# A gather that waits for the scores of an earlier tile: sparse graph attention on Trainium2

## The chip, the cores and the metric

The kernel runs on one core of a Trainium2 chip. It uses all five engines of that core: PE (matmul), DVE (vector), ACT (scalar), POOL (general purpose, and the issuer of every indirect DMA here) and SP (the issuer of the plain DMAs). The metric is the device time of one execution in microseconds (us), taken as the median of the runs. Times inside an execution are from one profiled execution and count from its first instruction.

## The reference

Four graph-attention layers follow each other, each as `x = x + layer(relu(layernorm(x)), adj)`. `x` is (8, 2048, 64): batch of 8, 2048 nodes, 64 channels. `adj` is 2048 x 2048 and sparse; its first rows are the densest. The change is in the third layer, which has four heads and then a second attention over the heads' output:

```python
def _gat_layer(h, mask, b):
    scores = jnp.einsum('...nd,...md->...nm', h, h)
    scores = jnp.where(mask, scores, NEG)
    attn = jax.nn.softmax(scores, axis=-1)
    return jnp.einsum('...nm,...md->...nd', attn, h) + b

mask = graph + jnp.eye(N, dtype=graph.dtype) > 0
h = jnp.einsum('bnc,hdc->bhnd', x, Wh)                 # 4 heads
out_h = _gat_layer(h, mask[None, None], bh[None, :, None, :])
z = leaky_relu(concat of the heads, 0.2)
h2 = jnp.einsum('bnk,dk->bnd', z, Wo)
out2 = _gat_layer(h2, mask[None], bo)                  # one head over h2
out = layernorm(leaky_relu(out2, 0.2)) * gamma + beta
```

Layer 1 (counted from 0) and layer 3 are additive attentions, layer 0 is a dot-product attention.

## The kernel before, in words

The kernel never forms a 2048 x 2048 score matrix. A first stage turns `adj` into lists of edges. The nodes are cut into 16 tiles of 128. A tile's edges are held in **slots** of 128 edges each: `ROWS[i]` slots in which partition p holds a neighbour of the tile's own node p, and then `PACKED[i]` slots into which the edges that are left over are packed, with a selection matrix that says which node each belongs to. One slot costs one **gather**: an indirect DMA that POOL issues (L256, in `gather`), which fetches 128 rows of 512 floats (8 batches x 64) from a table in HBM into one place of a ring of `RING = 26` places in SBUF. A tile has 3 to 16 slots, and all 16 tiles together have 76.

The stage of the change is called **the heads**: the first attention of layer 2. Its tiles are worked through in `ORDER2 = [8, 9, 12, 10, 13, 11, 3, 7, 5, 6, 2, 4, 0, 14, 1, 15]`. I write T13.0 for slot 0 of tile 13. `pipeline` runs five functions per tile, staggered by one tile each:

- `take2` issues the gathers of a tile (POOL), the load of its own rows (`rows<-table`, SP, L265), the load of its queries for four heads (`q<-qtab`, SP, L808, 1040 KB; the first two tiles have it in SBUF already), and the first loads of queries per packed edge (`qe<-qtab,qidx`, an indirect DMA of POOL, L797, 1040 KB; four buffers).
- `first2` calls `score` twice, once for the `ROWS` slots and once for the packed ones. For each slot ACT copies the gathered row to PSUM (L820), DVE multiplies it with the query (L822, 128x2048) and reduces the product (L826), a small DVE operation subtracts the self score (L827), and ACT takes the exponential (L828). A packed slot needs its `qe` load; the next `qe` load is issued when a packed slot's L827 is done.
- `second2` sums the weights by node (PE, L438), and for each half of the heads (k = 0, 1) POOL multiplies each gathered row with its weights (`wh`, L839; L855 adds two of them in some tiles; three buffers), and PE accumulates the result (`y`, L857), starting from the tile's own rows (L848). ACT divides (L869). After this the tile's ring places are free.
- `third2` and `fourth2` transpose, project and write the rows for the next attention (PE L898, L902, L914, L920; ACT L900, L481, L917, L922; DVE L482).

What stands in which order on each engine is decided by a list scheduler when the program is built: it estimates times for the operations and their dependencies, and emits one fixed sequence for each engine. On the chip each engine then runs its sequence in that order; an instruction whose semaphore isn't there yet holds all that stand behind it on that engine. So a new dependency changes not only when an instruction may start but also where it stands, and the places of others with it. A gather that needs a ring place waits for the operations that read the place's last content.

`gather` has an argument `behind`: an instruction that the **first** gather of the tile (slot 0) has to wait for. The two additive layers use it already, with the tile `SPREAD[k]` (2 or 3) ahead. The heads pass nothing.

Of the kernel before, what the change touches and what calls it, by code (L numbers as in the profile page):

```python
# [13 lines left out]
OP = mybir.AluOpType  # L14
AX = mybir.AxisListType
# [54 lines left out]
def edge_stack(ctx: ExitStack, tc: tile.TileContext, x_in, adj, w1, w1t, a1, wh, wht, bh, wo, bo,  # L70
# [9 lines left out]
    nc = tc.nc  # L80
# [127 lines left out]
    def heads(t, n=B):  # L208
        return t.rearrange("p (b d) -> p b d", b=n)
# [7 lines left out]
    order = list(MAKING)  # L217
# [13 lines left out]
    kept = {}  # L231
# [12 lines left out]
    def row(i, t):  # L244
        return ring[:, (held[i] + t) % RING, :F]

    taken = {}

    def gather(k, i, st, behind=None):

        n = SLOTS[i]
        assert sum(SLOTS[j] for j in held) + n <= RING
        held[i], front[0] = front[0], (front[0] + n) % RING
        cols = table[k].shape[1]
        for t in range(n):
            g = nc.gpsimd.indirect_dma_start(  # L256
                out=ring[:, (held[i] + t) % RING, :cols], out_offset=None, in_=table[k][:, :],
                in_offset=bass.IndirectOffsetOnAxis(ap=idx[:, OFF[i] + t:OFF[i] + t + 1], axis=0))
            if behind is not None and t == 0:
                tc.add_manual_dep(g.ins, behind.ins.name, mybir.DependencyInfo(  # L260
                    mybir.DependencyClass.Sync, mybir.DependencyReason.DATA), reason="gather")

    def load(st, name, src, bufs):
        st[name] = rows_pool[0].tile([P, F], F32, name=name, bufs=bufs)
        nc.sync.dma_start(out=st[name], in_=src)  # L265

    def rows_of(k, i):
        return table[k][i * P:(i + 1) * P, :F]
# [512 lines left out]
    with tc.tile_pool(name="l2", bufs=2) as l2p, \  # L781
# [10 lines left out]
        def fetch(upto):  # L792

            while len(sent) <= min(upto, len(stream) - 1):
                i, t = stream[len(sent)]
                q = sent[i, t] = l2p.tile([P, QW], F32, name="qe", bufs=QE)
                nc.gpsimd.indirect_dma_start(  # L797
                    out=q, out_offset=None, in_=qtab[:, :],
                    in_offset=bass.IndirectOffsetOnAxis(ap=qidx[:, POFF[i] + t:POFF[i] + t + 1], axis=0))

        def take2(i, st):
            gather(2, i, st)
            load(st, "rows", rows_of(2, i), 3)
            if i in order[:2]:
                st["q"] = kept[i]
            else:
                st["q"] = own_pool[0].tile([P, QW], F32, name="q")
                nc.sync.dma_start(out=st["q"], in_=qtab[i * P:(i + 1) * P, :])  # L808
            fetch(stream.index((i, 0)) + min(PACKED[i], QE) - 1)

        def score(i, st, lo, hi):

            K, n = ROWS[i], hi - lo
            w = l2p.tile([P, max(ROWS), B * H], F32, name="w2", bufs=5)[:, :n]
            st.setdefault("w", []).append(w)
            s = ps_s.tile([P, F], F32, name="s2")[:, :n * B * H].rearrange("p (t c) -> p t c", c=B * H)
            for t in range(lo, hi):
                q = st["q"] if t < K else sent[i, t - K]
                g = ps_g.tile([P, F], F32, name="g2")
                nc.scalar.copy(g, row(i, t))  # L820
                pr = l2p.tile([P, B * H, D], F32, name="prod2")
                nc.vector.tensor_tensor(  # L822
                    pr.rearrange("p (b h) d -> p b h d", h=H),
                    q[:, :B * H * D].rearrange("p (b h d) -> p b h d", h=H, d=D),
                    heads(g)[:, :, None, :].to_broadcast([P, B, H, D]), op=OP.mult)
                nc.vector.tensor_reduce(s[:, t - lo, :], pr, AX.X, OP.add)  # L826
                nc.vector.tensor_tensor(s[:, t - lo, :], s[:, t - lo, :], q[:, B * H * D:], op=OP.subtract)  # L827
                nc.scalar.activation(w[:, t - lo], s[:, t - lo], AF.Exp, bias=mbb[:, OFF[i] + t:OFF[i] + t + 1])  # L828
                if t >= K:
                    fetch(stream.index((i, t - K)) + QE)  # L830
# [41 lines left out]

        def first2(i, st):
            score(i, st, 0, ROWS[i])
            score(i, st, ROWS[i], SLOTS[i])

        def second2(i, st):
            d, p = by_query(i, st["w"], B * H)
            rec = st["rec"] = small.tile([P, B, H], F32, name="rec2")
            rf = rec.rearrange("p b h -> p (b h)")  # L880
            nc.vector.scalar_tensor_tensor(rf, p, 1.0, d, op0=OP.add, op1=OP.add)
            nc.vector.tensor_reduce(most2[:, i:i + 1], rf, AX.X, OP.max)
            nc.vector.reciprocal(rf, rf)
            for k in range(2):
                weights(i, st, k)
                divided(i, st, k)
            done(i, st)
# [42 lines left out]
    with tc.tile_pool(name="ps_q", bufs=3, space=bass.MemoryType.PSUM) as ps_q, \  # L930
# [88 lines left out]
        lo = small.tile([1, 1], F32, name="lo", bufs=1)  # L1019
# [514 lines left out]
```

## Time and profile before

| | |
|---|---|
| time, median of 3 runs | 1483.09 us |
| the three runs | 1474.09, 1483.09, 1483.28 us |
| the profiled execution | 1474.39 us, of which the span of its instructions is 1472.7 us |
| mean granted TensorE clock in it | 0.906 |
| busy in it | PE 1197.5 us, DVE 1153.7, POOL 1041.3, ACT 729.5 |
| gathers (L256), all layers | 380, mean 962 ns of POOL each |
| query loads per packed edge (L797) | 34, mean 963 ns of POOL each |
| `wh` products (L839) | 152, mean 1917 ns |
| score product and reduction (L822, L826) | 76 each, 2.28 us each |
| the heads, from the first gather to the last matmul | 529.9 to about 1053 us |

How to read it: POOL's 0.96 us for an indirect DMA is the time to issue it; the data land later, by semaphore. Busy time of PE is of pipelined matmuls, so a PE that is busy all the time needn't be at its peak. The window view gives for each stretch of time the busy time of each engine, the granted clock, the share of the 16 DMA engines that is busy, and what they move. The timeline gives single instructions in order, with the idle time before each and what ended it. The chain is the sequence of work that ended last, followed back from the end.

### The profile page before, as it was taken

The page shows a single profiled execution, that of the slowest core. Times are in us where ns is not written, and L with a number is a line of the kernel's source. Part 1 is how long each engine was busy: PE and PEld are TensorE (multiplying, and loading weights), DVE is VectorE, ACT ScalarE, POOL GpSimd, SP SyncE. Part 2 cuts the span into 40 slices and gives each one's busy share as a digit, 9 for nine tenths or more (in the row PEclk, how much of TensorE's full clock was granted, in tenths as well). Part 3 has the DMA queues.
Part 4 walks back from the last instruction along what each step waited for, and adds up shares of the span by engine and source line. Part 5 has one row for each costly group of instructions (what it writes and reads, how often), then busy time and mean ns, then how long its engine had stood idle before and what let it go on. Part 6 is the DMA issues. An engine that isn't in the chain of part 4 may idle for free.

```text
span 1472.7 us, 16011 instructions
## 1 busy us (share of the span) xinstructions
PE 1197.5 (81%) x4106; PEld 634.3 (43%) x4106; DVE 1153.7 (78%) x2267; ACT 729.5 (50%) x2467; POOL 1041.3 (71%) x851
## 2 busy tenths in 40 slices
PE   4757887957999852988999989988767798957997
PEld 1733444544554421444444434443333354555654
DVE  6978998735779896989888998951279999955765
ACT  5636677853445731666654654343524547741111
POOL 4646888857863558888787999987288689727640
PEclk9997999977999976999999999999868879957999
DMA  7767665537874578755455436200284453138861
GB/s 227 265 200 259 188 219 172 198 112 227 288 230 156 217 287 296 238 188 203 157 196 166 144 125 236 66 7 8 81 300 144 131 176 122 66 120 234 253 188 46
DMA packets 88621, 262.76 MB, mean 178 GB/s; under 512 B 14828, under 2 KB 16792, under 8 KB 80200
## 3 DMA queue, kind: packets, MB, share of 16 engines
q0 software_dynamic: 35680, 136.59, 29.6%
q1 hardware_dynamic: 52840, 125.06, 24.4%
q8 instruction: 35, 0.57, 0.2%
q14 instruction: 66, 0.54, 0.1%
HBM read 204.41 MB, written 57.18 MB: 178 GB/s over the span
## 4 chain that ended last, share of the span: by engine, by line
PE 29%; DVE 16%; POOL 7%; issue 6%; DMA 6%; ACT 5%; SPq 0%; DVEq 0%; POOLq 0%; ACTq 0%
PE y L857 9%; PE y L424 6%; DVE prod L822 4%; DVE s L826 3%; POOL g L256 3%; POOL wh L839 3%; PE y L848 2%; DMA g<-table,idx 2%; DMA rows<-table 2%; PE m L914 2%; PE m L902 2%; ACT yn L869 2%; DMA qe<-qtab,qidx 1%; PE q L606 1%; PE m L438 1%
## 5 line engine op out<-in xcount | busy, mean ns | idle before, releaser
L256 POOL DMA_INDIRECT g<-table,idx x380 | 365.4, 962 | 207.9 <-issue 80.3
L839 POOL TENSOR_TENSOR wh<-g,w 128x1024 f32<-128x1024 f32 x152 | 287.8, 1917 | 41.1 <-PE y L857 39.6
L424 PE MATMUL y<-wg,ident 128*128 128x512 f32 x336 | 192.5, 697 | 26.1 <-POOL wg L419 22.2
L826 DVE TENSOR_REDUCE s<-prod 128x32 f32<-128x2048 f32 x76 | 172.5, 2285 | 10.3 <-ACT w L828 10.1
L419 POOL TENSOR_TENSOR wg<-g,w 128x1024 f32<-128x1024 f32 (+1 forms) x86 | 146.6, 1719 | 31.7 <-ACT w L476 23.4
L857 PE MATMUL y<-wh,ident 128*128 128x512 f32 x272 | 133.9, 618 | 25.1 <-POOL wh L855 23.6
L424 PE MATMUL y<-wg,selt 128*128 128x512 f32 x272 | 141.0, 628 | 5.2 <-DVE wg L419 2.8
L857 PE MATMUL y<-wh,selt 128*128 128x512 f32 x272 | 128.4, 599 | 1.0 <-POOL wh L839 1.0
L869 ACT ACTIVATE yn<-y,rec 128x64 f32<-128x64 f32 x512 | 112.3, 370 | 23.6 <-DVE y L862 16.3
L424 PEld LDWEIGHTS y<-wg,ident 128*128 128x128 f32 x336 | 66.8, 217 | 97.5 <-issue 54.7
L419 DVE TENSOR_TENSOR wg<-g,w 128x1024 f32<-128x1024 f32 (+1 forms) x86 | 92.9, 1088 | 10.8 <-PE y L424 9.4
L438 PEld LDWEIGHTS m<-w,selt 128*128 128x128 f32 x408 | 63.6, 204 | 86.4 <-issue 23.7
L438 PE MATMUL m<-w,selt 128*128 128x8 f32 (+1 forms) x408 | 61.4, 255 | 47.3 <-ACT w L590 19.4
L822 DVE TENSOR_TENSOR prod<-q,g 128x2048 f32<-128x2048 f32 x42 | 95.6, 2276 | 3.0 <-ACT g L820 2.8
L468 PE MATMUL q<-rows,sel 128*128 128x512 f32 x136 | 80.9, 690 | 19.4 <-DVE prod L462 12.7
L822 DVE TENSOR_TENSOR prod<-qe,g 128x2048 f32<-128x2048 f32 x34 | 77.5, 2279 | 23.5 <-DMA qe<-qtab,qidx 16.8
L857 PEld LDWEIGHTS y<-wh,ident 128*128 128x128 f32 x272 | 52.1, 199 | 89.6 <-issue 57.7
L820 ACT COPY g<-g 128x512 f32<-128x512 f32 x76 | 47.6, 626 | 86.4 <-DVE prod L822 84.4
L424 PEld LDWEIGHTS y<-wg,selt 128*128 128x128 f32 x272 | 52.4, 205 | 60.1 <-issue 49.0
L902 PE MATMUL m<-att,whd 128*128 128x512 f32 x120 | 64.5, 619 | 15.0 <-ACT att L900 14.8
L857 PEld LDWEIGHTS y<-wh,selt 128*128 128x128 f32 x272 | 49.6, 190 | 60.8 <-issue 55.7
L482 DVE SCALAR_TENSOR_TENSOR zt<-m,bhc,att 128x512 f32<-128x512 f32 x60 | 44.4, 741 | 36.6 <-ACT att L481 36.6
(247 smaller groups left out, 2659.9 us busy)
## 6 DMA issues: line engine op xcount, KB each, us to landing
qtab<-q SPq DMA_DIRECT2D x16, 1040.0 KB, 4.8
a<-in_adj_dram SPq DMA_DIRECT2D x32, 512.0 KB, 5.0
q<-qtab SPq DMA_DIRECT2D x14, 1040.0 KB, 5.9
table<-xh SPq DMA_DIRECT2D x48, 256.0 KB, 3.7
rows<-table SPq DMA_DIRECT2D x48, 256.0 KB, 4.0
xs<-x SPq DMA_DIRECT2D x48, 256.0 KB, 2.5
x<-xs SPq DMA_DIRECT2D x48, 256.0 KB, 3.0
table<-xh SPq DMA_DIRECT2D x32, 260.0 KB, 2.4
```

The source lines that it names most:

```text
L256: g = nc.gpsimd.indirect_dma_start(out=ring[:, (held[i] + t) % RING, :cols], out_offset=None, in_=table[k][:, :], in_offset=bass.IndirectO ...
L419: eng.tensor_tensor(wg[:, :m].rearrange("p t (b d) -> p t b d", b=B), g[:, :, :F].rearrange("p t (b d) -> p t b d", b=B), w[:, t0:t0 + m, ...
L424: nc.tensor.matmul(y, lhs(i, t), wg[:, t - t0, :], start=(t == 0 and own is None), stop=(t == n - 1))
L438: nc.tensor.matmul(p[:, :cols], selt(i, t), packed[:, t, :], start=(t == 0), stop=(t == T - 1))
L468: nc.tensor.matmul(qe, sel(i, t - K), q, start=True, stop=True)
L820: nc.scalar.copy(g, row(i, t))
L822: nc.vector.tensor_tensor(pr.rearrange("p (b h) d -> p b h d", h=H), q[:, :B * H * D].rearrange("p (b h d) -> p b h d", h=H, d=D), heads(g ...
L826: nc.vector.tensor_reduce(s[:, t - lo, :], pr, AX.X, OP.add)
L839: nc.gpsimd.tensor_tensor(wg, heads(row(i, t))[:, :, None, :].to_broadcast([P, B, 2, D]), w[:, :, 2 * k:2 * k + 2, None].to_broadcast([P, ...
L857: nc.tensor.matmul(st["ys"][j], lhs(i, t), wg[:, 4 * j:4 * j + 4], start=first, stop=(t == n - 1))
L869: nc.scalar.activation(yn[:, b, h, :], st["ys"][j][:, b, h, :], AF.Copy, scale=st["rec"][:, 4 * j + b, 2 * k + h:2 * k + h + 1])
L902: nc.tensor.matmul(p, whd[j // 2], yt, start=True, stop=True)
```

## The change

In the heads, the first gather of a tile now waits for the scores of the tile that is four places ahead of it in `ORDER2`: for that tile's last reduction (L826) over its `ROWS` slots. Tiles 0 to 3 of the order wait for nothing more than before. The other gathers of a tile get no such wait. No operation is added or taken away, and no transfer changes its size.

```diff
         def take2(i, st):
-            gather(2, i, st)
+            n = order.index(i)
+            gather(2, i, st, taken[2, order[n - 4]] if n >= 4 else None)
             load(st, "rows", rows_of(2, i), 3)
...
-                nc.vector.tensor_reduce(s[:, t - lo, :], pr, AX.X, OP.add)
+                kept["s"] = nc.vector.tensor_reduce(s[:, t - lo, :], pr, AX.X, OP.add)
...
         def first2(i, st):
             score(i, st, 0, ROWS[i])
+            taken[2, i] = kept["s"]
             score(i, st, ROWS[i], SLOTS[i])
```

`gather` itself, unchanged, hangs the wait on slot 0 alone:

```python
            if behind is not None and t == 0:
                tc.add_manual_dep(g.ins, behind.ins.name, mybir.DependencyInfo(
                    mybir.DependencyClass.Sync, mybir.DependencyReason.DATA), reason="gather")
```

## The prediction

> **What bounds the kernel now.** The change touches one stage, so I looked for what holds that stage. First the window view, for the engines' load by stretch:
>
> ```profile
> core 0: us, PE busy (x) PEld busy (x) DVE busy (x) ACT busy (x) POOL busy (x), PEclk, DMA share, GB/s
> ...
> 558.00:571.00 13.00, 0.00 (x0) 0.00 (x0) 0.00 (x0) 0.00 (x0) 10.86 (x11) 0.50 0.94 345
> 571.00:600.00 29.00, 19.34 (x46) 8.86 (x46) 28.60 (x21) 10.91 (x38) 24.45 (x16) 0.82 0.66 233
> 600.00:625.00 25.00, 25.00 (x68) 10.77 (x68) 24.93 (x25) 15.41 (x57) 22.17 (x16) 1.00 0.74 255
> ```
>
> The reader is to see a hole: from 558 to 571 us PE, DVE and ACT do nothing at all; only POOL issues, and the DMA engines are 94% busy. After that PE and DVE are nearly full (600 to 900 us: PE 92 to 95%, DVE 88 to 94%, POOL 79 to 91%). The wait view of 500 to 620 us names the hole, and the chain of 556 to 592 us, in order of time, shows what it is made of:
>
> ```profile
> DVE prod L822 <- DMA qe<-qtab,qidx: 13.3, 1, 13.3
> ```
>
> ```profile
> 557.00 0.21 DVE s L827
> 557.21 0.29 issue
> 557.50 0.95 POOL g L256
> 558.45 0.30 issue
> 558.75 0.95 POOL g L256
> 559.70 0.30 issue
> 560.00 0.95 POOL g L256
> 560.95 0.30 issue
> 561.25 0.95 POOL g L256
> 562.21 0.30 issue
> 562.51 8.54 DMA qe<-qtab,qidx
> 571.05 0.02 issue
> 571.07 2.30 DVE prod L822
> ```
>
> POOL issues 26 gathers in a row (529.9 to 562.2 us, 1.25 us apart), until the ring's 26 places are used up, and only then the first `qe` load. DVE finished tile 8's three row slots at 557.2 and needs that load for slot T8.3. It lands 8.5 us after its issue began. Everything later in the heads hangs on this start.
>
> **What the change does to the order.** The orders of the two built programs show it on POOL: 22 gathers, then the four `qe` loads. T13.0, T11.0, T3.0 and T7.0 have left the opening run; T13.1, T13.2 and so on stay in it, since only slot 0 waits. T13.0 now stands between the second and third `wh` product of tile 8, T11.0 between T8.0 and T8.1 of its second half, T3.0 behind tile 8's last product, T7.0 before tile 12's third. Later slot 0s stand one to four places behind their sisters. DVE, ACT, PE and SP swap neighbours here and there, and in the next attention too. No work is added.
>
> **The opening.** Four gathers at 1.25 us are 5.0 us that the `qe` load gains on POOL: issue at 557.5 instead of 562.5. None of its semaphores holds it there: its youngest store to the query table was issued at 542.0, and it waits for a reduction ended at 541.9. What can take gain back is the landing. From 534 to 572 us the DMA engines are about full (0.82 to 1.02 in slices of 2 to 4 us), and SP issues a 1040 KB `q` load at 557.2, which the earlier `qe` load now has beside it from its first byte. The trace has no `qe` load at that instant; the five issued between 555 and 580 us landed in 6.2 to 11.1 us, median 9.8. So DVE resumes between 563.7 and 568.6, a gain of 7.4 to 2.5 us. I take the median of these neighbours: 557.5 + 9.8 = 567.3, a gain of **3.8 us**.
>
> The Trainium skill (DMA: Bandwidth & Descriptors, Anatomy of one DMA — SWDGE (gpsimd) path) fits an undisturbed load as 2.0 us plus bytes over 436 GB/s, an estimate of 4.4 us for these 1040 KB, where this trace shows 8.54; by it the gain would be 571.07 - 561.9, 9.1 us. The same page (Queues, rings and completion order) says that an engine takes turns between queues, packet by packet; that speaks against the full gain, as SP's load would get every other turn.
>
> **The gathers put back.** They cost 1.25 us of POOL each, in the middle of products. T13.0 stands ahead of the sum that PE's first product waits for: that sum ends 5.0 - 1.25 = 3.75 us earlier instead of 5.0 (575.15 now), which is what DVE gains anyway. T11.0: POOL's sum of T8.0 and T8.1 ends at 590.30, PE starts on it at 591.67, so 1.25 of 1.37 us slack are used. T8.3's product ends at 595.9, PE takes it at 597.4; still covered. T9.0's ends at 600.2 against 601.2 on PE, so up to 0.25 us late; the order lets POOL catch up one gather there (T6.0 stands later than before). T7.0 and T5.0 fall ahead of POOL's wait of 4.23 us for PE at 637.45. I take **0.3 us** for all of them; if POOL's cover were gone it would be 3 x 1.25 = 3.75 us, and below nothing isn't excluded by more than POOL's one spare gather, 1.25 us.
>
> **The waits added.** At a gather's new place, would POOL come before the reduction? By the timelines of before (reduction's end; POOL's arrival): T11.0 580.2; 583.0. T3.0 594.4; 595.9. T7.0 617.4; 619.9. T5.0 636.0; 633.6. T6.0 644.2; 645.6. T2.0 668.4; 669.6. T4.0 702.8; 700.1. So two waits, 2.4 and 2.7 us. Behind each stand gathers or `wh` products, and PE waits for these. But both fall where POOL sat idle for PE, 4.23 us at 637.45 and 4.89 us at 708.58, so they cost nothing; uncovered, 5.1 us. As DVE and POOL both move by about the same amount, the margins of 1.2 to 2.8 us should hold. From T0.0 on the pipeline's own waits come later than the new one.
>
> **The rest.** An earlier start passes through PE, full from 600 us on, to the end of the heads at 1053 us. PE's idle time between 571 and 1053 us is 37 us, and other places of `zt` (L482) on DVE may shift some of it. In the next attention DVE is 94 and 97% busy (1100 to 1200, 1200 to 1300 us), so another order there has 9 us of idle DVE time to gain or lose; SP's moved `q` load passes a `rows` load that isn't needed for some 40 us. I count all this as 0, within -3 to +3 us.
>
> **Sum:** -3.8 + 0.3 + 0 = **-3.5 us**. Against the profiled execution, 1474.39 - 3.5 = 1470.9 us. That execution agrees with the fastest of the three runs (1474.09); the other two are 9 us higher, at 1483.1 and 1483.3, without anything that the page could show of them. The predicted median carries the difference over: 1483.09 - 3.5 = **1479.6 us**.
>
> **Rivals.**
> 1. *The gain is swallowed.* POOL is 23.0 to 24.3 us busy of 25 from 825 to 975 us and has the same work as before, only moved; if the four gathers come back where POOL sets the pace, its end stays. For it: the high load there, and that POOL, with PE, ends the heads. Against: POOL idled 39.6 us waiting for `y` products between 565 and 1060 us, time that can hold 5. The same result if the `qe` load lands no earlier because DMA alone decides. 0 us: 1483.1.
> 2. *The load flies.* The `qe` load lands in 6.2 us, the shortest of its neighbours: -7.4 us, 1475.7. For it: four gathers, 1 MB, fewer in the rings ahead of it. Against: the `q` load beside it.
> 3. *Slower: POOL waits in front of products.* One mechanism, at T5.0 and T4.0 and at the margins under 1.5 us (T3.0, T6.0, T2.0): POOL, having lost its four opening gathers sooner than DVE regains its pace, reaches the gather before the reduction, and the products behind it come late to PE. Price: 2.4 + 2.7 us at the two, 3 x 1.25 us for gathers ahead of products, together 8.9, less the 3.8 of the opening: +5, 1488. It decides once PE has no stock of products left, that is, where POOL no longer waits for PE.
> 4. *It doesn't do what it says*, since other waits cover it: excluded at the opening by the built order; it is part of the first rival.
>
> **How the numbers follow.** Forecast 0.50, first rival 0.22, second 0.12, third 0.16. From the bounds, -7.4 on the faster group (1474.1) gives 1466.7, +5 on the slower group (1483.3) gives 1488.3; with the +-3 us of other orders I give 1466 to 1489. A measurement of this kernel can hardly tell less than 1% (14.8 us) from no change, and the runs themselves lie 9 us apart. Under -1% lies only the second rival in the faster group, and a little of the rest: 0.10. Over +1% lies none of the cases, only an accident of order larger than I can find: 0.08. Within: 0.82.
>
> **What would show it.** Right: 22 gathers ahead of the first `qe` load; DVE's wait for `qe` down from 13.3 to some 9.5 us; the last matmul of the heads 3 to 4 us earlier against the first gather; no wait of L256 for L826 above 3 us. Wrong: the wait for `qe` still 12 or more (DMA decides); POOL idle before L256 for L826 in several places and PE idle for `wh` grown by as much (third rival); heads equal and the difference in the next attention (orders).

## The result, and the profile after

The changed kernel is slower: 1491.1 us median (1479.25 to 1506.05) against 1479.21 us (1471.86 to 1491.39) for the kernel before, 20 runs each; the ratio is **1.0076, 95% interval 1.0050 to 1.0102**. It leaves out the longest run of the changed kernel (1506.05 us) as a slow one. The forecast was 3.5 us faster. The profiled execution of the changed kernel took 1499.93 us, its span 1498.2 us. That is near the upper end of its runs, and the profiled one of before (1474.39 us) is near the lower end: the two profiles differ by 25.5 us, twice what the medians do.

All lines from 803 on stand one to three lines lower in the changed kernel: the score product is L823, its reduction L827, the subtraction behind it L828, the `wh` product L840, `y` L858, and PE's L914 is L917.

The wait for the query load, in the wait view from 506 to 626 us (the heads start 5.8 us later in this execution, at 535.7 us, after stages whose order is the same in both kernels):

```profile
engine line waited for: us in total, times, longest us
...
DVE prod L823 <- DMA qe<-qtab,qidx: 8.8, 1, 8.8
```

The same instants on POOL, in its timeline:

```profile
start us, us, engine line op out<-in xcount [idle before <-releaser]
562.06 0.95 POOL L256 DMA_INDIRECT g<-table,idx  x1 [0.30 <-issue]
563.31 0.94 POOL L797 DMA_INDIRECT qe<-qtab,qidx  x1 [0.30 <-issue]
...
568.01 3.78 POOL L840 TENSOR_TENSOR wh<-g,w 128x1024 f32<-128x1024 f32 x2
```

The opening did what was forecast. The first `qe` load is issued 27.6 us after the first gather instead of 32.6, it lands 10.4 us later instead of 8.5, DVE's wait falls from 13.3 to 8.8 us, and the product of T8.3 starts 3.1 us earlier against the first gather. POOL's first product starts 5.0 us earlier, at 32.3 us instead of 37.3.

The windows that answer to those shown of before:

```profile
core 0: us, PE busy (x) PEld busy (x) DVE busy (x) ACT busy (x) POOL busy (x), PEclk, DMA share, GB/s
564.00:577.00 13.00, 0.00 (x0) 0.00 (x0) 3.77 (x5) 0.88 (x2) 11.89 (x9) 0.59 0.95 347
577.00:606.00 29.00, 23.39 (x52) 10.55 (x53) 28.13 (x26) 12.67 (x47) 23.62 (x18) 0.77 0.70 264
606.00:631.00 25.00, 24.02 (x63) 9.73 (x62) 24.56 (x21) 13.76 (x47) 19.16 (x13) 1.00 0.63 217
```

The second row holds the gain: PE does 52 matmul instructions in it where before did 46. The third row shows that it goes at once: PE does 63 instead of 68, and POOL is busy for 19.2 us instead of 22.2. POOL waits there. Its wait view over the whole heads, first of before (529.9 to 1060 us), then of the changed kernel (535.7 to 1072 us):

```profile
POOL wh L839 <- PE y L857: 39.6, 22, 4.9
```

```profile
POOL wh L840 <- PE y L858: 45.1, 23, 8.0
```

POOL does not wait for the scores that the change names: no gather of the heads has a wait for a reduction above 0.3 us. It waits longer for PE. Against the first gather, POOL's products stand 5.0 us earlier at tile 8, 0.5 us earlier at the end of tile 9, then 1.9 us later in the second half of tile 12, 4.1 us later in that of tile 11, 6.6 us later in that of tile 2, and so to the end. The stretch from the first gather of the heads to the first gather of the second attention is 535.7 us instead of 529.5. The second attention took 265.8 us instead of 260.8, the last layer 161.0 instead of 152.5.

### The profile page after: what moved, and what is told of

Same layout as the page of the kernel before. It is cut to its first block, busy times and chain, and to the rows that moved or that the text cites. A ratio compares the mean times of both kernels' runs of the same rounds, so it can differ in the third digit from the quotient of the medians.

```text
span 1498.2 us, 16006 instructions
## 1 busy us (share of the span) xinstructions
PE 1211.3 (81%) x4106; PEld 641.2 (43%) x4106; DVE 1149.7 (77%) x2267; ACT 728.9 (49%) x2467; POOL 1041.8 (70%) x851
## 5 line engine op out<-in xcount | busy, mean ns | idle before, releaser
L840 POOL TENSOR_TENSOR wh<-g,w 128x1024 f32<-128x1024 f32 x152 | 288.0, 1917 | 46.6 <-PE y L858 45.1
L424 PE MATMUL y<-wg,ident 128*128 128x512 f32 x336 | 190.4, 690 | 27.1 <-POOL wg L419 23.7
L827 DVE TENSOR_REDUCE s<-prod 128x32 f32<-128x2048 f32 x76 | 172.9, 2287 | 12.6 <-ACT w L829 12.4
L858 PE MATMUL y<-wh,ident 128*128 128x512 f32 x272 | 138.3, 636 | 19.2 <-POOL wh L856 17.8
L424 PE MATMUL y<-wg,selt 128*128 128x512 f32 x272 | 140.7, 627 | 5.1 <-DVE wg L419 4.3
L858 PE MATMUL y<-wh,selt 128*128 128x512 f32 x272 | 128.9, 600 | 0.0
L424 PEld LDWEIGHTS y<-wg,ident 128*128 128x128 f32 x336 | 66.7, 217 | 96.6 <-issue 54.7
L823 DVE TENSOR_TENSOR prod<-q,g 128x2048 f32<-128x2048 f32 x42 | 95.6, 2276 | 4.6 <-ACT g L821 4.4
L858 PEld LDWEIGHTS y<-wh,ident 128*128 128x128 f32 x272 | 53.3, 204 | 85.6 <-issue 58.1
L823 DVE TENSOR_TENSOR prod<-qe,g 128x2048 f32<-128x2048 f32 x34 | 77.4, 2277 | 15.2 <-DMA qe<-qtab,qidx 9.0
L424 PEld LDWEIGHTS y<-wg,selt 128*128 128x128 f32 x272 | 51.8, 203 | 58.8 <-issue 46.8
L858 PEld LDWEIGHTS y<-wh,selt 128*128 128x128 f32 x272 | 49.4, 190 | 61.9 <-issue 56.3
L482 DVE SCALAR_TENSOR_TENSOR zt<-m,bhc,att 128x512 f32<-128x512 f32 x60 | 44.4, 741 | 40.8 <-ACT att L481 40.7
```

What stands on the lines that cost most here:

```text
L424: nc.tensor.matmul(y, lhs(i, t), wg[:, t - t0, :], start=(t == 0 and own is None), stop=(t == n - 1))
L823: nc.vector.tensor_tensor(pr.rearrange("p (b h) d -> p b h d", h=H), q[:, :B * H * D].rearrange("p (b h d) -> p b h d", h=H, d=D), heads(g ...
L827: kept["s"] = nc.vector.tensor_reduce(s[:, t - lo, :], pr, AX.X, OP.add)
L840: nc.gpsimd.tensor_tensor(wg, heads(row(i, t))[:, :, None, :].to_broadcast([P, B, 2, D]), w[:, :, 2 * k:2 * k + 2, None].to_broadcast([P, ...
L858: nc.tensor.matmul(st["ys"][j], lhs(i, t), wg[:, 4 * j:4 * j + 4], start=first, stop=(t == n - 1))
```

## The experiments

### How they are made, and what is compared

The theory after this reading is **order** (theory O in the expectations): the waits cost nothing, but the scheduler, having them, gave all five engines other sequences, and these cost the time. Its rival is that the **waits** hold POOL back (theory W); a third possibility is that the single profiles differ by chance (theory V).

The experiments fix the sequence of every engine by hand. Before the scheduler runs, each instruction gets an ordering dependency, without a semaphore, on the one that is to stand ahead of it on its engine:

```diff
         nc.vector.tensor_scalar(flag, lo, -1.0, 1.0, op0=OP.mult, op1=OP.add)
+        pin(tc, nc)
...
+def pin(tc, nc):
+    ins = {int(i.name[2:]): i for i in nc.cur_bb.bb.instructions}
...
+        for a, b in zip(at, at[1:]):
+            tc.add_manual_dep(ins[b], ins[a].name, mybir.DependencyInfo(
+                mybir.DependencyClass.NoSync, mybir.DependencyReason.DATA), reason="order")
```

The traces show that this holds: on PE, DVE, ACT and POOL e_nowait runs the same sequence as the changed kernel, instruction by instruction, and e_open and e_qe run that of before on PE, DVE and ACT. That the fixing itself costs time is not seen: two such kernels, e_open and e_four below, are not slower than before. In these kernels lines stand three lower than in before (gather L259, `qe` load L800, product L825, `wh` L842, `y` L860). In e_poolwait, which keeps the change too, it is four from the change on, so L830 is there the score's reduction.

Two numbers are read from each run: the ratio of times, and the **heads**, the stretch of the profile from the first gather of the heads to the next table's first gather. Kernels were measured in five sets, with 4 to 12 runs of each kernel beside 17 to 31 of before: A 1477.3 us, B 1514.0, C 1516.6, D 1477.7, E 1479.1 (medians of before). In B and C everything was slower, before too: the layer ahead of the heads took 221 to 222 us there instead of 206 and the last layer 168 to 175 us with the order of before instead of 148 to 152. So times are compared within a set. The heads vary less: four profiles in A, D and E and the one of before, all with the order of before there, give 525.9 to 529.5 us, mean 527.6; one in C gives 525.9.

| run | set | T8.3's product | first `wh` | heads | ratio, 95% interval |
|---|---|---|---|---|---|
| before | | 41.2 | 37.3 | 529.5 | |
| changed | | 38.1 | 32.3 | 535.7 | 1.0076, 1.0050 to 1.0102 |
| e_nowait | A | 37.4 | 32.3 | 535.0 | 1.0127, 1.0078 to 1.0176 |
| e_heads | A | 38.8 | 32.3 | 535.2 | 1.0035, 1.0000 to 1.0070 |
| e_tail | A | 41.1 | 37.3 | 527.8 | 1.0109, 1.0078 to 1.0140 |
| e_open | A | 37.3 | 32.4 | 526.4 | 0.9985, 0.9957 to 1.0013 |
| e_pool | B | 37.3 | 32.3 | 559.6 | 1.0209, 1.0155 to 1.0262 |
| e_rest | B | 39.3 | 37.3 | 536.5 | 1.0053, 1.0028 to 1.0078 |
| e_poolwait | B | 37.1 | 32.3 | 564.5 | 1.0200, 1.0142 to 1.0258 |
| e_early | B | 26.7 | 25.2 | 515.9 | 0.9880, 0.9847 to 0.9912 |
| e_qe | C | 26.8 | 41.6 | 530.5 | 1.0067, 1.0031 to 1.0103 |
| e_place | C | 38.9 | 37.4 | 525.9 | 0.9960, 0.9925 to 0.9994 |
| e_dist6 | C | 37.9 | 34.8 | 524.1 | 1.0049, 1.0011 to 1.0088 |
| e_dist3 | C | 35.8 | 31.2 | 528.1 | 1.0060, 1.0020 to 1.0099 |
| e_att2 | D | 40.0 | 37.4 | 525.9 | 1.0018, 0.9985 to 1.0050 |
| e_last | D | 40.7 | 37.4 | 526.6 | 1.0035, 1.0010 to 1.0060 |
| e_four | D | 38.2 | 32.4 | 524.6 | 0.9962, 0.9934 to 0.9990 |
| e_lastfix | E | 40.4 | 37.4 | 527.9 | 1.0009, 0.9977 to 1.0041 |
| e_early2 | E | 26.7 | 25.0 | 513.3 | 0.9875, 0.9829 to 0.9922 |

All columns but the last are in us; the third and fourth count from the first gather of the heads.

### The order without the waits: e_nowait

The edit is the one above, with the changed kernel's sequences; the change itself is not in it.

> The edit: none of the change's eight waits is in it, but on each of the five engines every instruction of the program stands where the changed kernel has it (the order is fixed by hand). So it holds the order without the waits. Theory O (the waits cost nothing, the order that the scheduler made from them costs it): as the changed kernel, +12 us on before, ratio 1.005 to 1.010; from the first gather of the heads to the next table's first gather some 535 us, where before has 529.5 and the changed kernel 535.7. Theory W (the waits hold POOL back, and PE behind it): the opening's gain stays and the loss goes, -3 us, ratio 0.996 to 1.000, that stretch 526 us. Theory V (the two single profiles differ by chance, and the loss lies outside the heads): ratio near 1.008, but that stretch within 2 us of before's.

Measured: 1.0127, heads 535.0 us, and POOL's wait for PE in the heads is 45.1 us in 23 times, as in the changed kernel. Every jump comes back: the products of this run stay within 0.7 us of the changed kernel's all the way through the heads. The loss is there without a single one of the change's waits. So the waits fall as its cause, and so does chance.

### Heads or later layers: e_heads, e_tail

```diff
-e_nowait: PINNED = the changed kernel's sequences
+e_heads:  PINNED = the changed kernel's to the end of the heads, before's behind them
+e_tail:   PINNED = before's to the end of the heads, the changed kernel's behind them
```

> The edit: no waits; every engine in the changed kernel's order up to the end of the heads, and in the order of before in the second attention and the last layer. Theory O, in the form that the profiles suggest: the heads lose 6 us between their first gather and the next table's first gather, and the layers behind keep the time of before; +6 us, ratio 1.004. If the whole loss is made in the heads: +12, ratio 1.008. If the heads' loss was chance and the loss comes from the order behind them: -3 to 0 us, ratio 0.998 to 1.000. Theory W: the same -3 to 0, since there is no wait.

> The edit: no waits; the order of before up to the end of the heads, the changed kernel's order on every engine in the second attention and the last layer. Theory O with a share for the layers behind: the second attention 265 us instead of 260.8, +4 to +6 us, ratio 1.003 to 1.004. Theory O with all of it in the heads, and theory W: 0 us, ratio 0.999 to 1.001.

Measured: e_heads 1.0035, heads 535.2 us, 7.6 us over the mean of those with the order of before. e_tail 1.0109, heads 527.8 us. Both parts cost, and by these two runs **the larger part of the loss is made behind the heads**, in stages that the change does not name. The price of e_tail, 16 us, is more than either form of the theory gave.

### The opening alone: e_open

```diff
 POOL: 13 gathers (T8, T9, T12, T10)
-T13.0
 T13.1  T13.2
-T11.0
 T11.1  T11.2
-T3.0
 T3.1  T3.2  T3.3  T3.4
-T7.0
 T7.1, four qe loads, first wh product of tile 8, ...
+(the four stand where the changed kernel has them)
```

> The edit: no waits; the order of before on every engine, but the four gathers T13.0, T11.0, T3.0 and T7.0 leave the opening and stand on POOL where the changed kernel has them. So it is the opening of the prediction and nothing else. By the prediction's sum: vector engine's wait for the first qe load 9.5 us or less instead of 13.3, and 3.5 us off the end, ratio 0.9976. Theory O agrees: -3 us, stretch of the heads 526 to 527 us. The rival (what the opening wins is lost again in any case, because POOL gets the four gathers back where it sets the pace): 0 us, ratio 0.999 to 1.001, stretch 529 us or more.

Measured: heads 526.4 us, ratio 0.9985, which cannot be told from 1. DVE's wait for `qe` was 10.5 us, not 9.5 or less, and the product of T8.3 3.9 us earlier. POOL's first product is 4.9 us earlier than in before, but from tile 9 on the products are only 1.4 us earlier, to the end. (Five profiles with the order of before in the heads lie between 0.9 us earlier and 0.8 us later than the one of before over most of these products, so the 1.4 is a rough figure.) PE's first product is 3.7 us earlier: the gather T13.0 stands ahead of the sum that it needs. PE's timeline of this run shows where another 1.7 us or so went:

```profile
600.14 1.12 PE L860 MATMUL y<-wh,ident 128*128 128x512 f32 x2 [0.53 <-POOL wh L842]
602.00 1.13 PE L860 MATMUL y<-wh,selt 128*128 128x512 f32 x2 [0.74 <-POOL wh L842]
```

In before PE stands at neither place. These are tile 9's first products, which the gathers put back have delayed on POOL: counted from the first gather the two start 2.4 and 1.4 us earlier than in before.

### The place of the four gathers: e_four

```diff
 POOL: 22 gathers, T8.0 to T3.2
-T3.3  T3.4  T7.0  T7.1
 four qe loads, products of tile 8 ...
+T3.3 ... in the places that POOL has for gathers, in the order of the gathers,
+and four new places: three at 103 us and one at 161 us, where POOL waited for PE
```

> The edit: no waits, the order of before on every engine but POOL's gathers in the heads: the last four gathers (T3.3, T3.4, T7.0, T7.1) leave the opening, as many as the change takes out; the gathers keep their order, take the next places that POOL has for gathers, and four more places stand where POOL waited for PE (three at 103 us, one at 161 us from the first gather in the profile of before). The run with the change's own four put them in front of products and kept 1.4 us of the 4.9. If that place was the fault: POOL's first product 5 us earlier and the heads' last product too, 4.5 to 5.5 us off the heads, ratio 0.996 to 0.998. If PE or DVE takes it back anyway: 1 to 3 us, ratio 0.998 to 1.000.

Measured: ratio 0.9962, heads 524.6 us; POOL's first product 4.9 us earlier, its products 2.3 us earlier through most of the heads and 3.0 at the end. So better places keep some 1 to 1.5 us more than e_open's 1.4, which is near the scatter of such profiles; how much of e_open's loss is a matter of the places is not settled. The rest is lost at better places too.

### POOL's order alone, with and without waits: e_pool, e_poolwait, and the counterpart e_rest

```diff
+e_pool:     before's sequences, but POOL's in the heads are the changed kernel's
+e_poolwait: the same sequences, and the change itself with its waits
+e_rest:     before's sequences, but PE's, DVE's, ACT's and SP's in the heads are the changed kernel's
```

> The edit: no waits; in the heads POOL alone stands in the changed kernel's order (all its gathers, qe loads and products), every other engine, and every later stage, in the order of before. Known by now: with all engines in the changed order the heads take 535 us from their first gather to the next table's, with the order of before 527.8 to 529.5, with the opening alone changed 526.4. If POOL's order makes the loss (its later gathers stand in front of products that PE needs): 534 us or more, +5 us on the whole, ratio 1.003 to 1.005. If it is the order on PE, DVE and ACT: 526 to 528 us, ratio 0.997 to 1.000.

> The edit: as the run with POOL's order alone, but with the eight (of twelve) waits that the changed kernel's program holds, or as many as this order needs. So the pair shows the price of the waits with nothing else changed. The prediction's step (T5.0 and T4.0 wait where POOL would idle for PE anyway, the others come after the reduction): the same time and the same heads, within 1 us. Theory W (a wait of POOL makes products late): 2 to 5 us more, heads longer by the same, and waits of L256 on a reduction of several us in the trace.

> The edit: no waits; the counterpart: in the heads PE, DVE, ACT and SP stand in the changed kernel's order, POOL in that of before, with its 26 gathers ahead of the first qe load; every later stage in the order of before. If PE's, DVE's and ACT's order makes the loss: the opening's gain is missing too, so 536 to 539 us for the heads, ratio 1.005 to 1.007. If POOL's order makes it: 528 to 530 us, ratio 0.999 to 1.001. Something between, with the same in the run before, would say that it is made where the two meet.

Measured: e_pool 1.0209, heads 559.6 us, some 32 us longer than with the order of before: far beyond either expectation. e_rest 1.0053, heads 536.5 us, some 9 us longer, as expected if the order of PE, DVE and ACT makes a loss. Each half of the changed order costs by itself, and both together 8 us. So it is not one engine's sequence that is bad. The changed POOL order fits the changed orders of PE and DVE better than it fits those of before. The wait view of e_pool over the heads shows what a misfit is:

```profile
POOL qe L800 <- DVE row L445: 14.1, 3, 12.5
...
POOL qe L800 <- PE y L860: 4.8, 1, 4.8
```

POOL comes to a `qe` load whose buffer DVE frees only later in its own sequence, and everything behind the load stands 12.5 us. A wait of 8.2 us ahead of another `qe` load has no releaser in the profile.

The pair with the waits settles their price. In e_poolwait a gather does wait:

```profile
POOL g L259 <- issue: 16.3, 49, 3.5
...
POOL g L259 <- DVE s L830: 2.9, 1, 2.9
POOL qe L800 <- PE y L861: 1.5, 1, 1.5
```

The wait of 2.9 us for a reduction, and one of 3.5 us for which the profile names no releaser, are not in e_pool. In each case POOL stands for PE in e_pool instead: 2.9 us at the first place, of which nothing is left in e_poolwait, and 4.8 us just behind the second, of which 1.5 is left. The products of the two runs lie within 0.7 us of each other until the last two, and the ratios are the same, though four runs of each could not show less than 1%. A wait that falls where POOL would stand for PE costs nothing: this step of the prediction held.

The last two products come 3.3 us later in e_poolwait, and its heads are 4.9 us longer, where no more than 1 us had been expected. The traces put that down to PE's clock and not to the waits: ahead of these products PE pauses 3.44 us in e_pool and 3.43 us in e_poolwait, and in the 4 us that follow its granted clock is 1.00 in e_pool and 0.50 in e_poolwait (whose profiled execution is the longest of its four, 1564.6 us).

### What holds the start of the heads: e_early, e_qe, e_early2

```diff
 POOL, e_early: 15 gathers (T8.0 to T13.1)
+qe of T8.3
 T13.2
+three more qe loads
-T11.0 to T7.1 (ten gathers)
 products of tile 8 ...
+T11.0 ... in the places that POOL has for gathers, and ten new places where it
+waited 3 to 5 us for PE (three at 103, two at 161, three at 174, two at 232 us)
```

e_early2 is the same kernel in another set. In e_qe all 26 gathers stay in the opening and only the four `qe` loads move up, behind the 15th.

> The edit: no waits, the order of before on every engine but POOL's gathers in the heads: 16 gathers instead of 26 in the opening, with the first qe load after the 15th and three more after the 16th; the following gathers keep their order and take the next places that POOL has for gathers, and ten more places are given to them where POOL waited 3 to 5 us for PE in the profile of before (3, 2, 3 and 2 of them). If the opening holds the heads as the prediction said, DVE's wait for qe nearly vanishes and POOL's first product starts 10 us earlier: 8 to 12 us off the heads, ratio 0.992 to 0.995. If PE or DVE takes it back later, as it took 2 us of the 5 in the run with the opening alone: -3 to -5 us, ratio 0.997. If gathers that come 10 to 20 us before their use arrive late for DVE: no gain, or slower by up to 5 us.

> The edit: no waits, the order of before on every engine, but in POOL's opening the four qe loads stand behind the 15th gather instead of behind the 26th; all 26 gathers stay in the opening. It takes apart the early run (first product 12 us earlier, heads 13.6 us shorter): there the loads came earlier and ten gathers left the opening. If DVE's wait for qe is what holds the heads: T8.3's product 12 to 14 us earlier and the heads 8 us or more shorter, ratio 0.992 to 0.995. If it is POOL's run of thirty issues, which stands in front of its first product: DVE starts earlier all the same, but the heads gain 0 to 4 us, ratio 0.997 to 1.000.

> The edit: the early opening once more (16 gathers, the qe loads behind the 15th and the 16th, the ten gathers later), on another chip. If the start of POOL's products holds the heads: first product 12 us earlier than in the run before, heads 514 to 517 us, 10 to 13 us off the whole, ratio 0.990 to 0.994. If the first run's gain lay in that chip's slow gathers: ratio 0.996 to 1.000.

Measured: e_early 0.9880, e_early2 0.9875, heads 515.9 and 513.3 us: 14 us shorter in set E than the mean with the order of before, and kept to the end. e_qe, in which DVE has its load just as early, has heads of 530.5 us and a ratio of 1.0067. The timeline of POOL in e_qe:

```profile
583.74 0.94 POOL L259 DMA_INDIRECT g<-table,idx  x1 [2.06 <-DMA qe<-qtab,qidx]
587.24 0.94 POOL L259 DMA_INDIRECT g<-table,idx  x1 [2.55 <-DMA qe<-qtab,qidx]
...
591.95 5.64 POOL L842 TENSOR_TENSOR wh<-g,w 128x1024 f32<-128x1024 f32 x3
```

and that in e_early2:

```profile
554.14 0.95 POOL L800 DMA_INDIRECT qe<-qtab,qidx  x1 [0.48 <-issue]
...
559.15 0.94 POOL L800 DMA_INDIRECT qe<-qtab,qidx  x1 [0.30 <-issue]
560.11 5.64 POOL L842 TENSOR_TENSOR wh<-g,w 128x1024 f32<-128x1024 f32 x3
```

In e_qe the loads were early, but POOL stood 4.6 us for the landing of two of them, and its first product came 4.3 us later than in before (41.6 us from the first gather). The semaphores in the trace say why: POOL's indirect DMAs use eight in rotation, and each waits for the landing of the one issued eight before it; for these two gathers that was the third and the fourth `qe` load. The heads became no shorter (4.5 us longer than e_place's in the same set), although the product of T8.3 started 14 us earlier than in before. In e_early2 the first product starts at 25.0 us. **The heads follow POOL's first product; curing DVE's wait for the load does not help without it.** The gain of e_early is ten issues less in front of that product (20 instead of 30), with the ten gathers given back where POOL idled. This kernel beats both: 18.5 us under before in set E.

How much DVE's wait holds by itself is an estimate: from tile 9 on e_qe's products are 3.6 us later than in before, with a first product 4.3 us later, so without that delay some 0.7 us might have been gained, which is within the scatter. The other half was not tried: no run moves POOL's first product and leaves the load late. In before POOL stands for the load too, right behind its first sum, through the score of T8.3:

```profile
578.25 0.98 POOL L797 DMA_INDIRECT qe<-qtab,qidx  x1 [3.10 <-DVE s L827]
```

So e_early's gain may need both.

### Which later layer: e_att2, e_last, e_place, e_lastfix

```diff
+e_att2:    before's sequences, but the changed kernel's in the second attention
+e_last:    before's sequences, but the changed kernel's in the last layer
+e_place:   before's sequences, but in the last layer three DVE and six PE
+           operations stand behind a wait, as in the changed kernel
+e_lastfix: e_last, with these nine ahead of the wait again
```

> The edit: no waits; the second attention alone stands in the changed kernel's order, on every engine; the heads and the last layer in that of before. Known: with the later layers both in the changed order, 1.1% slower. If the second attention's order makes it (its stretch was 264 to 273 us with the changed order, 260 to 262 with that of before, at the same clock of 0.79 to 0.80): ratio 1.004 to 1.010, and the larger part of the two runs. If the last layer's does: 0.999 to 1.002.

> The edit: no waits; the last layer alone stands in the changed kernel's order; the heads and the second attention in that of before. If its order makes its longer time (154.7 to 161.0 us against 148.5 to 152.5 on the same chip): ratio 1.003 to 1.006. If that was the lower clock of its first 75 us (0.79 to 0.81 against 0.82 to 0.86) and nothing else: 0.998 to 1.002.

> The edit: no waits, the order of before everywhere but at one place of the last layer: three DVE operations (two L419, one L511) and six PE ones (two L424, four L315) that before runs while a tile's weights wait for a gather, 24 us after the layer's first gather, stand behind that wait, as in the changed kernel. If such places are what the changed order costs: the first L424 of them 8 us later than before, the products behind it 2 to 3 us later, the last layer +1 to +3 us against the 148.5 to 152.5 us that it has with the order of before; too little for the whole time, ratio 0.999 to 1.003. If the engines catch up: the last layer within 1 us of the run before.

> The edit: as the run with the last layer alone in the changed order, but at the one place (three DVE and six PE operations, 24 us after the layer's first gather) the order of before: they stand ahead of the wait for the gather again. If that place makes the layer's loss: last layer 148 to 152 us instead of 157.5, ratio 0.999 to 1.001 instead of 1.0035. If it makes a part: 153 to 156 us, 1.001 to 1.003. If the other places do: 156 us or more, 1.003 to 1.004.

Measured: e_att2 1.0018, not to be told from 1; e_last 1.0035, its last layer 157.5 us. Over the profiles in A, D and E and the two shown above, the last layer takes 147.5 to 152.5 us with the order of before (six of them) and 154.7 to 161.0 with the changed order (four): no overlap, means 149.9 and 157.7. The second attention takes 259.7 to 265.3 with the order of before (seven) and 257.5 to 272.7 with the changed one (four); its own price stays open.

The place that e_place and e_lastfix move shows how another order costs time, though not how much. PE's timeline of the last layer in before, then in e_last:

```profile
1344.20 1.13 PE L424 MATMUL y<-wg,ident 128*128 128x512 f32 x2 [0.60 <-DVE wg L419]
1345.17 1.02 PE L424 MATMUL y<-wg,selt 128*128 128x512 f32 x2
1346.02 0.60 PE L315 MATMUL q<-ident,att 128*128 128x128 f32 x4
1350.34 2.30 PE L438 MATMUL m<-w,selt 128*128 128x8 f32 x10 [3.72 <-ACT w L561]
1352.50 2.05 PE L424 MATMUL y<-wg,selt 128*128 128x512 f32 x2
```

```profile
1346.45 1.88 PE L427 MATMUL y<-wg,selt 128*128 128x512 f32 x4
1355.53 2.30 PE L441 MATMUL m<-w,selt 128*128 128x8 f32 x10 [7.20 <-ACT w L564]
1357.69 2.05 PE L427 MATMUL y<-wg,ident 128*128 128x512 f32 x2
1359.53 1.61 PE L427 MATMUL y<-wg,selt 128*128 128x512 f32 x2
1360.98 0.60 PE L318 MATMUL q<-ident,att 128*128 128x128 f32 x4
```

Both wait for the same weights, whose gather lands late. In before PE does two products and four transposes first and waits 3.72 us. In e_last these stand behind the wait: PE stands 7.20 us, then does them at a clock that has fallen (0.74 granted in those 20 us, 0.83 in before). e_lastfix brings the nine back (the first product on time again, 0.1 us from before), and has a last layer of 155.7 us and a ratio of 1.0009. That would be a part, with the other places making the rest; but 155.7 lies among the four of the changed order, and the ratio's interval overlaps that of e_last, so it is not shown. e_place shows no loss, 0.9960, but proves little: in sets B and C gathers came so late that the nine ran about 20 us later with the order of before too (in e_rest, e_dist6 and e_qe), so the place was covered there.

### Other distances: e_dist6, e_dist3

```diff
-            gather(2, i, st, taken[2, order[n - 4]] if n >= 4 else None)
+            gather(2, i, st, taken[2, order[n - 6]] if n >= 6 else None)
```

and likewise with 3. Here the scheduler is free.

> The edit: the change as it is, scheduler and all, but a tile's first gather waits for the scores of the tile six ahead instead of four. Two gathers instead of four leave the opening; the built order differs from before's in the heads in few places (6 on POOL, 19 on PE), in the second attention in many (139 on DVE), in the last layer in none but one. If the orders make the time: heads 526 to 530 us, second attention 263 to 270 us instead of 260 to 261.7, last layer as before; ratio 1.000 to 1.005. If the waits themselves did, it would lie at 0.998 to 1.000, since these come later still.

> The edit: the change as it is, scheduler and all, but a tile's first gather waits for the scores of the tile three ahead instead of four. The built order has the changed kernel's places on PE and ACT in the last layer (8 others on DVE), an order of its own in the second attention (138 moves on DVE against the changed kernel's, 121 against before's) and in the heads. If the orders make the time: last layer 4 to 9 us longer than before's on the same clock, second attention anything from -2 to +10 us, heads 530 to 538 us; ratio 1.004 to 1.013. If the waits make it, these shorter distances wait longer than the changed kernel's, and waits of L256 on a reduction of several us stand in the trace: heads over 538 us.

Measured: e_dist6 1.0049 with heads of 524.1 us, 1.8 us less than e_place in the same set; e_dist3 1.0060 with heads of 528.1 us, below its expectation. With six tiles' distance the heads' order is nearly that of before and the heads are not longer, and still the whole is slower. The loss may lie in the second attention, which got another order and took 270.6 us; but with the order of before it took 265.0 us (e_place) and 268.1 (e_qe) in the same set, so this is not shown. Nor is the last layer's share in e_dist3: 170.3 us, where e_dist6 has 168.1 and e_qe 174.9. With three tiles' distance POOL's longest wait in the heads for the scores' reduction is 0.6 us: shorter distances did not bring longer waits.

## Why the prediction was wrong

**The opening: right.** Wait for `qe` 13.3 to 8.8 us (forecast 9.5), T8.3's product 3.1 us earlier (forecast 3.8). The load took 10.4 us from its issue, against the 9.8 that was taken from its neighbours. The fit that the prediction quoted from the Trainium skill (DMA: Bandwidth & Descriptors, Anatomy of one DMA — SWDGE (gpsimd) path) gave an estimate of 4.4 us; beside SP's load and the gathers in flight the trace gives more than twice that.

**"Everything later in the heads hangs on this start": wrong.** The prediction read DVE's longest wait as the bound. e_qe took that wait away, at the price of a later start of POOL, and gained nothing; e_early, which also lets POOL make its first product 12 us earlier, gained 12 to 14 us in the heads. The chain of before had run through DVE there, and the two starts are close: the load landed at 571.05 us, POOL's first sum ended at 575.15. PE's own longest wait in before points at POOL's sum:

```profile
PE y L857 <- POOL wh L855: 23.6, 4, 21.6
```

**Gathers put back, 0.3 us: too small.** As the prediction counts, from DVE's gain, e_open keeps 1.4 of 3.9 us, so the term is 2.5; from POOL's 4.9 it is 3.5, near the upper bound of 3.75. At tile 9 PE stood for POOL's products.

**Waits added, nothing: right.** e_nowait against the changed kernel and e_poolwait against e_pool. In the changed kernel neither of the two waits that were forecast, 2.4 and 2.7 us, shows.

**"The rest ... I count all this as 0, within -3 to +3 us": the step that failed.** It measured about +9 us in the heads (e_open's 526.4 us against 535.0 to 535.7 with all engines reordered) and, behind the heads, 5 us for the last layer's order and 16 us for both later layers together. The prediction had seen that instructions "swap neighbours here and there, and in the next attention too"; it had not counted them, and it does not speak of the last layer. Its bound for the next attention, 9 us of idle time on DVE, limits what a better order can gain there, not what a worse one can lose. In the second attention at least 142 of 393 DVE operations and 68 of 387 on PE have moved, in the last layer 33 of 308 and 30 of 307. Each list was the scheduler's answer to estimated times; none knew which gather would really come late.

In the heads the mechanism can be read at tile 12. PE in the changed kernel:

```profile
624.97 1.12 PE L849 MATMUL y<-rows,ident 128*128 128x512 f32 x2 [0.97 <-ACT yn L870]
625.93 1.02 PE L858 MATMUL y<-wh,ident 128*128 128x512 f32 x2
626.79 1.02 PE L858 MATMUL y<-wh,selt 128*128 128x512 f32 x2
627.74 1.07 PE L917 MATMUL m<-zt,wo 128*64 128x512 f32 x2
628.75 1.12 PE L858 MATMUL y<-wh,selt 128*128 128x512 f32 x2
629.71 1.02 PE L849 MATMUL y<-rows,ident 128*128 128x512 f32 x2
630.57 1.02 PE L858 MATMUL y<-wh,ident 128*128 128x512 f32 x2
```

and POOL in the changed kernel:

```profile
631.74 5.65 POOL L840 TENSOR_TENSOR wh<-g,w 128x1024 f32<-128x1024 f32 x3 [3.54 <-PE y L858]
```

PE reads each `wh` product twice, once for the first four of the eight batches and once for the other four, into two `y` tiles. In the changed kernel it finishes one `y` tile of tile 12 with all three products before it begins the other (at 629.71), so the first of the three `wh` buffers is free only when the matmul at 630.57 has read it; POOL stands 3.54 us for it. In before PE reads two products into the one `y` tile, the same two into the other, and then the third:

```profile
619.27 1.13 PE L848 MATMUL y<-rows,ident 128*128 128x512 f32 x2
620.23 1.02 PE L857 MATMUL y<-wh,ident 128*128 128x512 f32 x2
621.09 1.02 PE L857 MATMUL y<-wh,selt 128*128 128x512 f32 x2
621.95 1.02 PE L848 MATMUL y<-rows,ident 128*128 128x512 f32 x2
622.80 1.02 PE L857 MATMUL y<-wh,ident 128*128 128x512 f32 x2
```

```profile
622.95 0.98 POOL L797 DMA_INDIRECT qe<-qtab,qidx  x1 [1.20 <-DVE row L442]
623.98 3.78 POOL L839 TENSOR_TENSOR wh<-g,w 128x1024 f32<-128x1024 f32 x2
```

There POOL's next product, at 623.98 us, did not wait for PE at all; POOL had only stood 1.20 us for DVE ahead of a query load. This is the first of the three jumps; the other two were not followed to their instructions.

**The rivals.** The third, POOL waiting in front of products, had the right sign and the wrong cause: the products were late for PE's sequence, not for the new waits. By its cause, what happened is the "accident of order larger than I can find". The 0.08 for it was the chance of more than +1%, though; the measured +0.76% lies within the 1% that got 0.82, in the direction that was not forecast.

**The range.** 1466 to 1489 does not follow from its own terms: 1466.7 and 1488.3, each with the 3 us of other orders, give 1463.7 to 1491.3, which just holds the measured 1491.1. That would have been luck, since the rest was larger than 3 us. The faster and the slower group, on which the bounds were built, were three runs; the 20 runs of before are spread from 1471.9 to 1491.4 us.

**What stays open.** The parts do not add up exactly. e_heads, e_att2 and e_last cost 5.2, 2.7 and 5.2 us, together 13, near the 11 us of the changed kernel; but e_tail alone costs 16, where e_att2 and e_last together give 8. Whether the orders of two successive layers hurt each other, or the intervals (some 5 us wide to each side) hide it, was not settled. Nor was it settled how much of the last layer's 8 us is the sequence itself and how much the lower clock that comes with it (0.78 to 0.81 in its first 75 us with the changed order, 0.82 to 0.86 with that of before).

## What to carry to other kernels

A new dependency in a program that a list scheduler orders is two changes: the wait, and a new sequence on every engine from there to the end. Price the second by counting the moved instructions in every later stage, and try the change with the old sequences held fixed, before the wait itself is judged. And when several engines stand at a start, ask which one the full engine behind them waits for: here PE waited for POOL's first product, and taking work from in front of that and from in front of DVE's load was worth 18 us, where curing DVE's visible 13 us wait at the price of a later start of POOL was worth nothing.

## What was not expected of the hardware

- Executions repeat their order effects closely. Three kernels with the same sequences in the heads gave 535.7, 535.0 and 535.2 us, with the same jumps at the same products; the six with the order of before gave 525.9 to 529.5 us. So differences of 4 us or more in this stage can be read from single profiles, though the whole time scatters by 20 us.
- POOL stood behind its own indirect DMAs: in e_qe two gathers waited 2.06 and 2.55 us until a `qe` load had landed, although a gather uses nothing of it. This is the program's doing, by the eight semaphores in rotation. In before, where the 26 gathers stand ahead of the loads, the DMA eight places ahead of each but the first eight is a gather, and the gaps between issues are 0.30 us.
- After a pause PE can be slow for some microseconds: in the last layer of before two L424 matmul groups of the same shape took 1.02 us ahead of the wait of 3.72 us, at a granted clock of 1.00, and 2.05 us behind it, at 0.50. The Trainium skill (TensorE: Matmul & The Clock Gate, What's actually happening) has the clock halved after an idle window of about 3.4 us, which agrees with this pair. Near that length the same pause goes either way here: 1.00 after 3.44 us in e_pool, 0.50 after 3.43 us in e_poolwait. So a badly placed wait can be paid twice, once in idle time and once in clock.
